# Four residual graph layers on one core: seven-block left products in one more gated step, another split of normalisation and masking between engines

## The chip, the cores and the metric

The kernel runs on one core of a Trainium2 chip. The core has a matrix engine (TensorE, in the profile PE, with its weight loads as PEld), three engines for elementwise work (VectorE or DVE, ScalarE or ACT, GpSimd or POOL) and a queue engine, SyncE or SP, which here issues nearly all DMA transfers. The engines run side by side, each through its own list of instructions in order, and wait for each other by semaphores. The metric is the device time of one launch in microseconds, median of several runs.

## The reference

The input is a batch of 64 graphs, each with 256 nodes of 128 features, and one symmetric 256 x 256 adjacency matrix that they share, all in float32. Four layers follow each other, each as x = layernorm(x + layer(x)):

```
layer 0: h = x Wo; e = leaky(u1[idx1] + u2[idx2]);  att = softmax over rows where adj > 0;  out = att h + x Wself
layer 1: h = x W;  e = leaky(e_src[i] + e_dst[j]);  masked to adj plus the diagonal; softmax; out = elu(att h)
layer 2: five gated steps: m = adj h; z, r = sigmoid(gates of m and h); hv = tanh(w5 m + u5 (r h)); h = (1-z) h + z hv
layer 3: y = x K0 + (adj x) K1 + (adj^2 x) K2 + (adj^3 x) K3, with both adjacency branches equal
```

What matters here: in layer 1, exponentials are multiplied by a mask of zeros and ones before they are used; layer 2 multiplies by the adjacency from the left once in each of its five steps (numbered 0 to 4); each layer ends in a normalisation without learned factors.

## The kernel before

Two graphs make a unit; there are 32 units (`u` from 0 to 31), each with a 128 x 1024 slab of node features in four blocks of 128 nodes x 128 features (two graphs, two node chunks each). Ten lanes of buffers hold ten units at a time. When a unit has gone through all four layers, its lane takes up the next unit.

The order of the work is written by a planner at build time. Every operation is added with an engine and an assumed duration in ns (`add(DVE, 1150, ...)`); the planner plays the engines forward, gives each free engine the ready operation of least rank, and so fixes one list for each engine. The rank is the unit's number times `PERIOD` plus the operation's due time, and the due time grows along the unit's own chain with a factor: `PACE_GATED` in layer 2 and `PACE` in the other layers. The eight PSUM banks are handed out by the same planner. On the chip each engine runs its list in order, however long its operations really take.

Layer 1 (`layer1`) gets the row scores on all partitions by a DMA through DRAM (L543; by transposes for the first three units), makes the scores with ScalarE (L714), takes exponentials over 1024 columns in place (L717), multiplies them by `mask1` (L718, into `p`), and multiplies by X on TensorE (L725).

Layer 2 (`layer2`) needs for each step the left product of the adjacency with the current state. It has two forms. `left` (L771) is four products of 256 columns, two for each graph. `left_fast` gets the same result from seven products of 128 columns, one for each of seven block combinations of the state (built by VectorE at L781, L783, L784 into `s`, which lies in the buffer `e`) and of the matrix (`adjTf`, built once), with products at L788; one product is copied out by ScalarE (L800) and the rest is added up by VectorE at L815, L818, L820 and L821 into `m`. After `left`, ScalarE copies the result to `m` instead (L839). Which steps take which form is in `FAST`, and the step's input must have come in node order by DMA (`far`); of units 0 and 1 and of the last unit some steps do not qualify. The gates (L843) are products of 512 columns, then ScalarE takes tanh (L854, L862, L871) and VectorE combines (L857, L869, L873, L875). VectorE operations with two tensors in SBUF as inputs, such as these four, recur through the whole layer. The new state is turned to node order by a VectorE transpose of 32 x 32 blocks and two sets of DMAs (L883 to L889).

The normalisation (`layernorm`) takes statistics on VectorE (L566, L568), the power -1/2 on GpSimd (L571), and then scales each of the four blocks. From unit `TIGHT` = 4 on, and in the layers of `NORM`, ScalarE does this (L584), for which VectorE prepares a shift (L575, not in layer 0); else VectorE does it (L592, or L588 in layer 0). In layer 3 (`layer3`) the results lie in two PSUM banks, one for each node chunk; the last three units store each chunk by a DMA of its own (L955).

Functions that the change touches, and what calls them:

Of the kernel before, what the change touches and what calls it, by code (L numbers as in the profile page):

```python
# [18 lines left out]
LEAD = 10  # L19
BANKS = 8  # L20
BL = 32
FAST = (2, 3, 4)
NORM = (0, 1, 2, 3)
SCALES = True
TIGHT = 4
FIRST_FAR = {0: 2, 1: 2}
# [1 line left out]
PERIOD = 43e3  # L28
TAIL = 0.3
LATE = 6  # L30
PACE = 2.9
PACE_GATED = 1.56
HOLD = 80
DIRECT_ROWS = 3
# [28 lines left out]
class Plan:  # L63
# [47 lines left out]
    def run(self, spawn, units, key):  # L111
# [22 lines left out]
        def start(lane):  # L134
            mine = [u for u in queue if u % LANES == lane]
            if mine:
# [5 lines left out]
                for t in self.tasks[seen:]:  # L142
                    t.due = max([d.due + (PACE_GATED if t.layer == 2 else PACE) * (d.ns + (
                        d.wait + self.LATENCY["sp" if d.dma else d.eng] if d.dma or d.eng != t.eng else self.OWN[t.eng]))
# [52 lines left out]
def kernel(  # L197
# [28 lines left out]
    nc = tc.nc  # L226
    B, N, D = x.shape
    NC = N // P
    UB = 2
    NU = B // UB  # L230
    T = UB * N
    G = UB * NC
    PE, DVE, ACT, POOL = "pe", "dve", "act", "pool"
# [13 lines left out]
    add = plan.add  # L247

    def bank():
        return Cell(bank=True)  # L250

    def mm_ns(cols, n=1):
        return n * (cols * 1.667 + 5)
# [163 lines left out]
    for t, wT, n in ((wx0, woT, C0), (ws0, wselfT, D + 2)):  # L417
        ps = bank()
# [81 lines left out]
    def bn(ap):  # L500
        return ap.rearrange("p (b n) -> p b n", b=UB)
# [54 lines left out]
                ps.ap[:, g * P : (g + 1) * P], view()[:, g : g + 1].to_broadcast([P, P]), ident.ap), (src, ident), (ps,))  # L556
        return ps, lambda: ps.ap.rearrange("q (b c p) -> q b c p", b=UB, c=NC)

    def layernorm(u, L, pairs, swap=False, centred=False):

        st, ve, rstd = L["st"], L["ve"], L["rstd"]
        sts, xs = object(), object()
        for k, (c, view) in enumerate(pairs):
            add(DVE, 330, lambda k=k, view=view: nc.vector.bn_stats(st.ap[:, k, :], view().rearrange("p j d -> p d j")),  # L566
                (c,), (st,), group=sts)
        add(DVE, 150, lambda: nc.vector.tensor_scalar(  # L568
            ve.ap.rearrange("p (k j) -> p k j", k=2), st.ap.rearrange("p k (j s) -> p k j s", j=2)[:, :, :, 2], 1.0 / D, EPS,
            op0=ALU.mult, op1=ALU.add), (st,), (ve,))  # L570
        add(POOL, 1050, lambda: nc.gpsimd.tensor_tensor(rstd.ap, ve.ap, nhalf.ap, op=ALU.pow), (ve, nhalf), (rstd,))  # L571
        by_act = u >= TIGHT and plan.layer in NORM

        if by_act and not centred:
            add(DVE, 120, lambda: nc.vector.scalar_tensor_tensor(  # L575
                ve.ap.rearrange("p (k j) -> p k j", k=2), st.ap.rearrange("p k (j s) -> p k j s", j=2)[:, :, :, 1], -1.0,
                rstd.ap.rearrange("p (k j) -> p k j", k=2), op0=ALU.mult, op1=ALU.mult), (st, rstd), (ve,))
        for k, (c, view) in enumerate(pairs):
            for j in range(2):
                b, ch = (j, k) if swap else (k, j)  # L580
                at = slice(2 * k + j, 2 * k + j + 1)
                shift, col = (ones, slice(0, 1)) if centred else (ve, at)
                if by_act:
                    add(ACT, 400, lambda j=j, b=b, ch=ch, view=view, at=at, shift=shift, col=col: nc.scalar.activation(  # L584
                        X[u].ap[:, b, ch, :], view()[:, j, :], AF.Identity, bias=shift.ap[:, col], scale=rstd.ap[:, at]),
                        (c, shift, rstd), (X[u],), group=xs)
                elif centred:
                    add(DVE, 260, lambda j=j, b=b, ch=ch, view=view, at=at: nc.vector.tensor_scalar(  # L588
                        X[u].ap[:, b, ch, :], view()[:, j, :], rstd.ap[:, at], 1.0, op0=ALU.mult, op1=ALU.add),
                        (c, rstd), (X[u],), group=xs)  # L590
                else:
                    add(DVE, 260, lambda k=k, j=j, b=b, ch=ch, view=view, at=at: nc.vector.tensor_scalar(  # L592
                        X[u].ap[:, b, ch, :], view()[:, j, :], st.ap[:, k, 3 * j + 1 : 3 * j + 2], rstd.ap[:, at],
                        op0=ALU.subtract, op1=ALU.mult), (c, st, rstd), (X[u],), group=xs)
# [113 lines left out]
    def layer1(u, L):  # L708
        H = D + 1
        esd, e, p = L["esd"], L["e"], L["p"]  # L710
        es, ev = on_all(u, L["m"], L["row"], esd, lambda: esd.ap[:, 0])
        for g in range(G):
            b = g // NC
            add(ACT, 600, lambda g=g, b=b: nc.scalar.activation(  # L714
                e.ap[:, g, :].rearrange("p (c n) -> p c n", c=NC), ev()[:, b], AF.Prelu, bias=esd.ap[:, 1, g : g + 1], alpha=0.2), (es, esd), (e,), group=es)
        ef, pf = e.ap.rearrange("p g n -> p (g n)"), p.ap.rearrange("p g n -> p (g n)")
        add(ACT, 950, lambda: nc.scalar.activation(ef, ef, AF.Exp), (e,), (e,))  # L717
        add(DVE, 1150, lambda: nc.vector.tensor_mul(  # L718
            p.ap.rearrange("p (b c) n -> p b (c n)", b=UB), e.ap.rearrange("p (b c) n -> p b (c n)", b=UB),
            mask1.ap.rearrange("p (o c) n -> p o (c n)", o=1).to_broadcast([P, UB, NC * N])), (e, mask1), (p,))  # L720

        ps_x, px = bank(), L["xT0"]
        for b in range(UB):
            for jc in range(NC):
                add(PE, mm_ns(N), lambda b=b, jc=jc: nc.tensor.matmul(  # L725
                    ps_x.ap[:, b * N : (b + 1) * N], X[u].ap[:, b, jc, :], p.ap[:, b * NC + jc, :],
                    start=(b == 0 and jc == 0), stop=(jc == NC - 1), skip_group_check=True), (X[u], p), (ps_x,))
        add(ACT, 500, lambda: nc.scalar.copy(px.ap, ps_x.ap), (ps_x,), (px,))
        rs, hp, hn, th = L["rs"], L["ht"], L["m"], L["th"]
        ex, parts = L["ex"], object()  # L730
        for b in range(UB):
            ps_o = bank()

            def ov(ps_o=ps_o):
                return ps_o.ap[:, 0 : NC * H].rearrange("p (c k) -> p c k", c=NC)

            for ic in range(NC):
                add(PE, mm_ns(H), lambda b=b, ic=ic, ov=ov: nc.tensor.matmul(  # L738
                    ov()[:, ic, :], bn(px.ap)[:, b, ic * P : (ic + 1) * P], wx1.ap,
                    start=(ic == 0), stop=True, skip_group_check=True), (px, wx1), (ps_o,))  # L740
            r = rs.ap[:, b * NC : (b + 1) * NC].rearrange("p (c o) -> p c o", o=1)
            add(DVE, 120, lambda r=r, ov=ov: nc.vector.reciprocal(r, ov()[:, :, D : D + 1]), (ps_o,), (rs,), group=parts)
            for c in range(NC if SCALES and u >= TIGHT else 0):
                add(ACT, 290, lambda b=b, c=c, ov=ov: nc.scalar.activation(
                    gd(hp.ap)[:, b * NC + c, :], ov()[:, c, 0:D], AF.Copy, scale=rs.ap[:, b * NC + c : b * NC + c + 1]),
                    (ps_o, rs), (hp,), group=parts)
            if not SCALES or u < TIGHT:
                add(DVE, 350, lambda b=b, r=r, ov=ov: nc.vector.tensor_mul(
                    gd(hp.ap)[:, b * NC : (b + 1) * NC, :], ov()[:, :, 0:D], r.to_broadcast([P, NC, D])), (ps_o, rs), (hp,), group=parts)
        if not u:  # L750
            plan.rank = NU
            warm(6, [plan.tasks[-1]])
            plan.rank = None

        add(DVE, 330, lambda: nc.vector.tensor_scalar_min(hn.ap, hp.ap, 0.0), (hp,), (hn,))
        add(ACT, 550, lambda: nc.scalar.activation(th.ap, hn.ap, AF.Tanh, scale=0.5), (hn,), (th,))
        add(ACT, 550, lambda: nc.scalar.activation(ex.ap, hn.ap, AF.Exp), (hn,), (ex,))
        xf = X[u].ap.rearrange("p b c d -> p (b c d)")
        add(DVE, 600, lambda: nc.vector.scalar_tensor_tensor(hp.ap, hp.ap, 0.0, xf, op0=ALU.max, op1=ALU.add),
            (hp, X[u]), (hp,))  # L760
        add(DVE, 600, lambda: nc.vector.scalar_tensor_tensor(th.ap, ex.ap, 1.0, th.ap, op0=ALU.add, op1=ALU.mult),
            (ex, th), (th,))
        add(DVE, 600, lambda: nc.vector.tensor_add(hp.ap, hp.ap, th.ap), (hp, th), (hp,))
        layernorm(u, L, y_pairs(hp))


# [56 lines left out]
    def layer2(u, L):  # L823
        h, ht = turned(u, L, -1), X[u]
        for step in range(STEPS):
            m, at = L["m"], len(plan.tasks)
            fast = step in FAST and far(u, step - 1)
            ps_m = None if fast else bank()
# [94 lines left out]
    def layer3(u, L):  # L923
# [7 lines left out]
        ps = [bank() for _ in range(NC)]  # L931

        def view(c):
            return ps[c].ap.rearrange("p (k b d) -> p k b d", k=2, b=UB)
# [9 lines left out]
        for c in range(NC):  # L944
            for mc in range(NC):
                add(PE, mm_ns(N), lambda c=c, mc=mc: nc.tensor.matmul(  # L946
                    ps[c].ap[:, 0:N], a2T.ap[:, mc, c * P : (c + 1) * P], s.ap[:, mc * N : (mc + 1) * N],
                    start=False, stop=(mc == NC - 1), skip_group_check=True), (a2T, s), (ps[c],))
        layernorm(u, L, [(ps[c], lambda c=c: view(c)[:, 0]) for c in range(NC)], swap=True)
        if u < NU - 3:  # L950
            add("sp", 450, lambda: nc.sync.dma_start(out_u[u], X[u].ap), (X[u],), ())
            return
# [53 lines left out]
```

The softmax here doesn't subtract the row's maximum and nothing guards it: scores larger than these inputs give would overflow.

## Time and profile before

| | |
|---|---|
| device time, median of 3 runs | 1408.14 us (1408.05 to 1408.65) |
| span of the profiled execution | 1406.5 us (this run: 1408.72 us) |
| TensorE clock granted, mean | 0.997 |
| TensorE busy | 1396.0 us, 6163 instructions |
| VectorE busy | 1135.0 us, 2746 instructions |
| ScalarE busy | 939.2 us, 2125 instructions |
| GpSimd busy | 142.4 us, 134 instructions |
| DMA | 146.96 MB, 104 GB/s over the span |

The page gives one profiled execution. A row of the groups reads: line, engine, operation, output and inputs, shapes and count; then the total of its durations in us and the mean of one in ns; then the idle time of that engine just before these operations, and what ended it. Durations of successive operations on one engine overlap a little, so the totals of an engine's rows can exceed its busy time: VectorE starts 512-column operations 0.61 us apart that are recorded with 0.68 us. A float32 product is recorded as two TensorE instructions. A row of waits reads: who waited for whom, us in total, times, the longest. A row of the timeline reads: start, duration, engine, line, operation, and how many in a row.

### The profile page before, as it was taken

The page shows a single profiled execution, that of the slowest core. Times are in us where ns is not written, and L with a number is a line of the kernel's source. Part 1 is how long each engine was busy: PE and PEld are TensorE (multiplying, and loading weights), DVE is VectorE, ACT ScalarE, POOL GpSimd, SP SyncE. Part 2 cuts the span into 40 slices and gives each one's busy share as a digit, 9 for nine tenths or more (in the row PEclk, how much of TensorE's full clock was granted, in tenths as well). Part 3 has the DMA queues.
Part 4 walks back from the last instruction along what each step waited for, and adds up shares of the span by engine and source line. Part 5 has one row for each costly group of instructions (what it writes and reads, how often), then busy time and mean ns, then how long its engine had stood idle before and what let it go on. Part 6 is the DMA issues. An engine that isn't in the chain of part 4 may idle for free.

```text
span 1406.5 us, 20482 instructions
## 1 busy us (share of the span) xinstructions
PE 1396.0 (99%) x6163; PEld 961.8 (68%) x6163; DVE 1135.0 (81%) x2746; ACT 939.2 (67%) x2125; POOL 142.4 (10%) x134
## 2 busy tenths in 40 slices
PE   8999999999999999999999999999999999999998
PEld 8866666676666676676666677676666666666776
DVE  7988888879878788878788788888768888988642
ACT  5797647547766677757677778887766555566454
POOL 0110001001011001011000111021000000101011
PEclk9999999999999999999999999999999999999999
DMA  4213545454554445555445554545554443455411
GB/s 118 61 48 85 120 95 116 100 118 100 132 117 109 97 100 120 121 118 116 99 99 121 126 114 102 114 111 116 116 120 93 107 110 82 116 119 116 110 49 50
DMA packets 533246, 146.96 MB, mean 104 GB/s; under 512 B 460688, under 2 KB 498320, under 8 KB 533136
## 3 DMA queue, kind: packets, MB, share of 16 engines
q1 hardware_dynamic: 532336, 145.13, 46.6%
q8 instruction: 50, 0.82, 0.2%
q14 instruction: 60, 0.49, 0.1%
q10 hardware_dynamic: 800, 0.52, 0.1%
HBM read 81.10 MB, written 64.46 MB: 103 GB/s over the span
## 4 chain that ended last, share of the span: by engine, by line
PE 98%; DVE 1%; ACT 1%; DMA 0%; issue 0%; POOL 0%; SPq 0%; POOLq 0%; ACTq 0%; DVEq 0%
PE ps L843 48%; PE ps L771 12%; PE ps L788 10%; PE ps L939 8%; PE ps L695 4%; PE ps L725 4%; PE ps L946 4%; PE ps L690 2%; PE ps L619 2%; PE ps L738 2%; PE ps L344 0%; DMA m<-row 0%; PE ps L512 0%; PE ps L908 0%; ACT e L714 0%; PE ps L555 0%
## 5 line engine op out<-in xcount | busy, mean ns | idle before, releaser
L843 PE MATMUL ps<-m,gT 128*128 128x512 f32 x960 | 462.4, 593 | 0.4 <-DVE m L821 0.3
L571 POOL TENSOR_TENSOR rstd<-ve,nhalf 128x4 f32<-128x4 f32 x128 | 141.7, 1108 | 1258.9 <-DVE ve L568 1127.3
L843 PEld LDWEIGHTS ps<-m,gT 128*128 128x128 f32 x960 | 173.0, 190 | 124.9 <-issue 102.3
L862 ACT ACTIVATE e<-ps,bias 128x512 f32<-128x512 f32 x160 | 109.9, 688 | 119.4 <-PE ps L843 116.9
L854 ACT ACTIVATE e<-ps,bias 128x512 f32<-128x512 f32 x160 | 109.9, 688 | 84.8 <-PE ps L843 83.7
L843 PE MATMUL ps<-e,u5T 128*128 128x512 f32 x320 | 163.3, 592 | 0.0
L871 ACT ACTIVATE p<-ps,bias 128x512 f32<-128x512 f32 x160 | 109.7, 686 | 41.0 <-PE ps L843 38.5
L771 PE MATMUL ps<-adjT,x 128*128 128x256 f32 x512 | 135.1, 379 | 0.0
L873 DVE SCALAR_TENSOR_TENSOR p<-e,p 128x512 f32<-128x512 f32 x160 | 109.2, 683 | 23.7 <-ACT p L871 22.9
L788 PEld LDWEIGHTS ps<-adjTf,ht 128*128 128x128 f32 x546 | 88.0, 191 | 47.6 <-issue 38.4
L771 PEld LDWEIGHTS ps<-adjT,x 128*128 128x128 f32 x512 | 93.2, 190 | 35.2 <-issue 25.6
L788 PEld LDWEIGHTS ps<-adjTf,e 128*128 128x128 f32 x728 | 95.3, 192 | 15.0 <-issue 12.4
L788 PE MATMUL ps<-adjTf,e 128*128 128x128 f32 x728 | 102.9, 275 | 0.0
L843 PEld LDWEIGHTS ps<-e,u5T 128*128 128x128 f32 x320 | 59.8, 190 | 58.8 <-issue 45.0
L843 PE MATMUL ps<-xT,gT 128*128 128x512 f32 x192 | 97.8, 593 | 0.0
L788 PE MATMUL ps<-adjTf,ht 128*128 128x128 f32 x546 | 91.9, 274 | 0.0
L839 ACT COPY m<-ps 128x512 f32<-128x512 f32 x69 | 40.2, 583 | 70.6 <-PE ps L771 69.7
L857 DVE SCALAR_TENSOR_TENSOR e<-e,xT 128x512 f32<-128x512 f32 x96 | 65.7, 684 | 22.8 <-ACT e L854 22.1
L714 ACT ACTIVATE e<-m,esd 128x256 f32<-128x256 f32 x116 | 83.1, 763 | 0.9 <-DMA m<-row 0.9
L525 DVE STREAM_TRANSPOSE p<-x 128x512 f32<-128x512 f32 x61 | 67.1, 1100 | 15.1 <-ACT x L584 14.7
L695 PEld LDWEIGHTS ps<-ht,p 128*128 128x128 f32 x512 | 66.5, 190 | 12.1 <-issue 11.0
L566 DVE BATCH_NORM_STATS2 st<-ps 128x6 f32<-128x256 f32 x128 | 50.9, 421 | 25.2 <-PE ps L946 19.6
(174 smaller groups left out, 2640.4 us busy)
## 6 DMA issues: line engine op xcount, KB each, us to landing
hb<-p SPq DMA_DIRECT2D x182, 256.0 KB, 2.4
ht<-hb SPq DMA_DIRECT2D x484, 64.0 KB, 2.6
xT<-hb SPq DMA_DIRECT2D x244, 64.0 KB, 2.7
m<-row SPq DMA_DIRECT2D x58, 256.0 KB, 4.0
hb<-p SPq DMA_DIRECT2D x124, 64.0 KB, 1.8
ht<-hb SPq DMA_DIRECT2D x31, 256.0 KB, 3.2
out_dram<-x SPq DMA_DIRECT2D x29, 256.0 KB, 2.5
m<-in_x_dram SPq DMA_DIRECT2D x96, 64.0 KB, 2.7
```

Source lines behind the costliest of these rows:

```text
L525: add(DVE, 1050, lambda: nc.vector.transpose(v.ap.rearrange("p (a g i) -> p g a i", g=G, i=BL), X[u].ap.rearrange("p b c (j a) -> p (b c) ...
L571: add(POOL, 1050, lambda: nc.gpsimd.tensor_tensor(rstd.ap, ve.ap, nhalf.ap, op=ALU.pow), (ve, nhalf), (rstd,))
L695: add(PE, mm_ns(D + 2), lambda b=b, ic=ic, kc=kc, yv=yv: nc.tensor.matmul(yv()[:, ic, :], p.ap[:, b * NC + kc, ic * P : (ic + 1) * P], h.a ...
L714: add(ACT, 600, lambda g=g, b=b: nc.scalar.activation(e.ap[:, g, :].rearrange("p (c n) -> p c n", c=NC), ev()[:, b], AF.Prelu, bias=esd.ap ...
L771: add(PE, mm_ns(N), lambda b=b, mc=mc: nc.tensor.matmul(ps.ap[:, b * N : (b + 1) * N], lhs(b, mc), mat.ap[:, mc, :], start=(mc == 0), stop ...
L788: add(PE, mm_ns(P) + 4, lambda: nc.tensor.matmul(ps.ap[:, at * P : (at + 1) * P], lhs(), mat.ap[:, k, c * P : (c + 1) * P], start=True, st ...
L843: add(PE, mm_ns(T), lambda: nc.tensor.matmul(ps.ap, w(), rhs.ap, start=start, stop=stop, skip_group_check=True), (c, rhs), (ps,), after)
L854: add(ACT, 600, lambda ps_g=ps_g, up=up: nc.scalar.activation(r.ap, ps_g.ap, AF.Tanh, bias=bias2.ap[:, 1:2], scale=0.5 / up), (ps_g, bias2 ...
L862: add(ACT, 600, lambda ps_g=ps_g, up=up: nc.scalar.activation(z.ap, ps_g.ap, AF.Tanh, bias=bias2.ap[:, 0:1], scale=0.5 / up), (ps_g, bias2 ...
L871: add(ACT, 600, lambda ps_v=ps_v, up=up: nc.scalar.activation(v.ap, ps_v.ap, AF.Tanh, bias=bias2.ap[:, 2:3], scale=1 / up), (ps_v, bias2), ...
L873: add(DVE, 600, lambda: nc.vector.scalar_tensor_tensor(v.ap, z.ap, 1.0, v.ap, op0=ALU.add, op1=ALU.mult), (v, z), (v,))
L939: add(PE, mm_ns(N), lambda k=k, src=src, c=c, b=b: nc.tensor.matmul(view(c)[:, :, b, :], bn(src.ap)[:, b, c * P : (c + 1) * P], w3.ap[:, k ...
```

## The change

Five things change; nothing else does.

- `FAST` gains step 1: that step's left product takes the seven-block form wherever its input qualifies, as steps 2, 3 and 4 do already.
- `NORM` loses layer 1: the scaling at the end of layer 1 goes from ScalarE to VectorE in units 4 to 31, and the preparation of a shift for ScalarE goes away there.
- In layer 3 of units 29, 30 and 31 the first of the two node chunks is scaled by VectorE and the second by ScalarE (`last`); before, both were scaled by ScalarE.
- The multiplication by `mask1` in layer 1 goes from VectorE to GpSimd, with an assumed 2300 ns in place of 1150.
- `PACE` goes from 2.9 to 2.8. As the planner orders everything anew, all lists shift. Behind the edit, line numbers are higher by two.

```diff
-FAST = (2, 3, 4)
-NORM = (0, 1, 2, 3)
+FAST = (1, 2, 3, 4)
+NORM = (0, 2, 3)
...
-PACE = 2.9
+PACE = 2.8
...
-    def layernorm(u, L, pairs, swap=False, centred=False):
+    def layernorm(u, L, pairs, swap=False, centred=False, last=False):
...
         for k, (c, view) in enumerate(pairs):
+
+            act = by_act and (k or not last)
             for j in range(2):
...
-                if by_act:
+                if act:
                     add(ACT, 400, lambda j=j, b=b, ch=ch, view=view, at=at, shift=shift, col=col: nc.scalar.activation(
...
-        add(DVE, 1150, lambda: nc.vector.tensor_mul(
+        add(POOL, 2300, lambda: nc.gpsimd.tensor_mul(
             p.ap.rearrange("p (b c) n -> p b (c n)", b=UB), e.ap.rearrange("p (b c) n -> p b (c n)", b=UB),
             mask1.ap.rearrange("p (o c) n -> p o (c n)", o=1).to_broadcast([P, UB, NC * N])), (e, mask1), (p,))
...
-        layernorm(u, L, [(ps[c], lambda c=c: view(c)[:, 0]) for c in range(NC)], swap=True)
+        layernorm(u, L, [(ps[c], lambda c=c: view(c)[:, 0]) for c in range(NC)], swap=True, last=u >= NU - 3)
```

## The prediction

> **What bounds the kernel now.** I read the page first: busy shares, then the chain that ended last.
>
> ```profile
> PE 1396.0 (99%) x6163; PEld 961.8 (68%) x6163; DVE 1135.0 (81%) x2746; ACT 939.2 (67%) x2125; POOL 142.4 (10%) x134
> ...
> PE 98%; DVE 1%; ACT 1%; DMA 0%; issue 0%; POOL 0%; SPq 0%; POOLq 0%; ACTq 0%; DVEq 0%
> ```
>
> TensorE is both the busiest engine and 98% of the chain, so what shortens its instruction stream should shorten the span, unless another engine starts to make it wait. A busy PE is no proof of a PE at its peak, so I then looked at the list of waits for PE alone. It has three entries, 4.0 us together, and one matters:
>
> ```profile
> PE ps L725 <- DVE p L718: 2.3, 1, 2.3
> ```
>
> That is unit 0's mask at 29.7 us. After the first 30 us PE waits once, for 0.3 us. Next, the timeline of PE in the body, for the pitch (start to next start) of the two kinds of left product; the first column is the start, the second the time to the modelled end:
>
> ```profile
> 512.28 1.06 PE L788 MATMUL ps<-adjTf,e 128*128 128x128 f32 x8
> 513.17 0.62 PE L619 MATMUL ps<-wx,xT 128*128 128x133 f32 x4
> ...
> 525.18 1.89 PE L771 MATMUL ps<-adjT,x 128*128 128x256 f32 x8
> 526.91 1.03 PE L771 MATMUL ps<-adjTp,ht 128*128 128x256 f32 x4
> ```
>
> Eight 256-column instructions take 526.91-525.18 = 1.73 us (0.216 each); eight 128-column ones 513.17-512.28 = 0.89 us (0.111 each). Every float32 product of the program is two PE instructions in these records. Then the groups that the change touches:
>
> ```profile
> L771 PE MATMUL ps<-adjTp,ht 128*128 128x256 f32 x240 | 64.9, 379 | 0.0
> L718 DVE TENSOR_TENSOR p<-e,mask 128x1024 f32<-128x1024 f32 x32 | 38.9, 1216 | 4.4 <-ACT e L717 4.4
> L584 ACT ACTIVATE x<-ht,ve,rstd 128x128 f32<-128x128 f32 x112 | 48.9, 485 | 20.4 <-DVE ve L575 20.4
> L571 POOL TENSOR_TENSOR rstd<-ve,nhalf 128x4 f32<-128x4 f32 x128 | 141.7, 1108 | 1258.9 <-DVE ve L568 1127.3
> ```
>
> Last, because work goes to GpSimd, the timeline of POOL and DVE around the longest POOL operation:
>
> ```profile
> 1197.46 3.09 POOL L571 TENSOR_TENSOR rstd<-ve,nhalf 128x4 f32<-128x4 f32 x1 [30.49 <-DVE ve L568]
> ...
> 1197.20 0.68 DVE L873 SCALAR_TENSOR_TENSOR p<-e,p 128x512 f32<-128x512 f32 x1
> 1197.81 0.68 DVE L914 TENSOR_TENSOR m<-ht,x 128x512 f32<-128x512 f32 x1
> 1198.41 0.68 DVE L875 SCALAR_TENSOR_TENSOR p<-p 128x512 f32<-128x512 f32 x1
> 1199.01 0.68 DVE L869 SCALAR_TENSOR_TENSOR p<-e,xT 128x512 f32<-128x512 f32 x1
> ```
>
> This power of 4 elements has a median of 1.007 us; here it took 3.09 us and ended 0.9 us after the fourth of four DVE operations with two SBUF inputs. 31 of the 128 took over 1.1 us, and each of the 31 began beside such a DVE operation.
>
> **What the skill says.** (1) "SBUF — State Buffer", Who interferes with whom: a VectorE instruction with two SBUF inputs and a GpSimd instruction that reads SBUF share a read interface; the one that starts second is blocked until the first ends. The trace agrees for GpSimd waiting (rows above); for VectorE waiting it shows nothing[...]. (2) "GPSIMD Engine Reference", 3.1: a float32 tensor_tensor with two inputs costs about 2.6 cycles an element, 4497 ns for 2048. My estimate from it for 1024 elements: 2.25 us. No row shows one. (3) "TensorE: Matmul & The Clock Gate", Part 1: TensorE falls to half clock after an idle window. The trace agrees: after the 2.26 us wait the eight L725 instructions take 3.23 us, not 1.73.
>
> **The change part by part**, against the profiled span of 1406.5 us; the three timed runs (1408.05 to 1408.65) lie 1.6 to 2.2 us above it, so I take differences in the span and add them to 1408.1.
>
> *Seven-block product at step 1.* Units 0 and 1 keep the old form, so 30 units change, and the built order confirms it: the 120 adjTp products (x240 instructions) all go, the adjTf ones rise by 210. Per unit eight instructions, 1.73 us, become fourteen of 0.111, 1.56 us: 0.17 us less, x30 = 5.1 us. With the pitch of the two groups of four nearby (0.110 to 0.1125) it is 4.7 to 5.7. Fourteen weight loads in place of eight cost nothing further: the 0.111 was measured with them. Since PE is the chain, this counts in full: -5.1.
>
> Beside it VectorE gets seven operations per unit, rows L781, L783, L784, L815, L818, L820, L821: 413+283+284+420+413+281+411 = 2.5 us, x30 = +75.2 us. ScalarE loses 30 copies L839 (583 ns) and gains 30 of L800 (266): -9.5 us.
>
> *Normalisation of layer 1 on VectorE.* ScalarE loses row L584 x<-ht, 48.9 us; VectorE gains 112 of L592 x<-ht at 336 ns, +37.6, and loses 28 of L575 at 153 ns, -4.3. Per unit the path from rstd to X loses a hop and goes from 4 x 0.49 to 4 x 0.34 us; I credit nothing, since PE does not wait there.
>
> *Mask on GpSimd.* VectorE loses 38.9 us; GpSimd gains 32 x 2.25 = 72 us, to 214 us (15%).
>
> VectorE sum: 75.2+37.6-4.3-38.9+2.4 (tail, below) = +72 us of durations. All VectorE rows sum to 1282 us for 1135 busy, as successive operations overlap, so +72 becomes about +64 busy: 1199 us, 86% of 1401. ScalarE falls by about 61 us of durations. VectorE gets close but stays below PE.
>
> *Two-engine normalisation of units 29 to 31.* At the end ScalarE does four L584 in 1.50 us after rstd, then the store. Two go to VectorE (0.40 each, from PSUM), two stay (0.75 us), side by side: about -0.7 on the very end. Bounds 0 and -1.0.
>
> *Start.* Unit 0's exponentials end at 27.49; VectorE was busy with L660 until 28.4 and ended the mask at 29.63. GpSimd is free at 27.5 and ends at about 29.8 to 30: +0.3. Bounds -0.5 and +2, as the half clock may last longer. The two L619 products that now stand before L725 fill part of the wait.
>
> *Queues.* No DMA is added and SP gets the same transfers. On POOL the powers of other units now stand behind 2.25 us masks; ScalarE and VectorE wait for them, with PE two steps away. The planner counts GpSimd at 2.3 us, so it orders around it. PACE 2.8 reshuffles priorities everywhere: no row prices this; I take 0, bounds -1.5 and +2.
>
> *New waits for VectorE.* While a mask reads, the next two-input VectorE operation may be blocked. They fill 669 us of the span, about half, so one comes within some 0.6 us: a block of up to 2.25-0.6 = 1.6 us, x32 = 53 us more on VectorE (then 89% on average). What stands behind it is VectorE's whole queue. From the trace, the time between a VectorE result and the PE instruction that reads it: last add of a seven-block product (L821) to the gate product, median 1.27 us, lower quartile 1.08; reset gate (L857) to its product, median 2.4, lower quartile 1.8. So most blocks are absorbed, some are not. In the likeliest case I charge a few short stalls, +1.2 us; bounds 0 and +11 (below).
>
> Sum: -5.1 -0.7 +0.3 +1.2 = -4.3 us, so 1403.8.
>
> **Rivals.** (A) *GpSimd blocks VectorE and PE pays, slower.* Each block of 1.6 us meets an L821 whose slack is the median 1.27: 0.33 us of stall, x32 = 10.6 us; 1408.1-5.1-0.7+0.3+10.6 = 1413. It decides from 5.5/32 = 0.17 us of PE stall per mask for a loss at all, 0.26 for one of 0.2%. For it: the read interface is shown to be shared, and VectorE is 83 to 88% busy from 100 to 1300 us. Against it: reset gates have more slack, VectorE has idle gaps before L815 and L869 that swallow part, and a mask falls near an L821 only sometimes. (B) *The saving is half eaten.* The 30 new chains of dependent additions and tighter mask results (L718 to L725 had slack under 1.25 us in a quarter of cases) cost PE 0.1 us each, 30+32 times = 6 us less some luck; time about 1407. (C) *The fourteen smaller products save nothing*, because weight loads bound them: 1408. The measured pitch excludes it almost wholly.
>
> **How the numbers follow.** A change below 0.2% (2.8 us) can't be told from none: faster is below 1405.3, slower above 1411.0. Likeliest case 58%, its own range 1401.5 to 1405.3; B with C 18%; A 24%. The range leaves out the far part of A and the luckiest reshuffles: 1400.8 to 1412.5. Faster 0.57, same 0.19, slower 0.24.
>
> **What would show it.** Right: adjTf group at 14 x 121 = 1694 instructions with the 0.111 pitch, adjTp gone from the left products, PE busy near 1391 us, waits of PE still a few us, last ScalarE group of two instead of four. L720's mean on POOL near 2.3 us confirms the price; 3 us and more would mean that it waits for VectorE. Wrong towards A: two-input VectorE rows (L859, L871, L875, L877 after) of 512 columns with maxima near 2 us where before none passed 0.73, and a list of PE waits with tens of entries for m L823, e L859 or p L720. Wrong at the start: a wait of PE at L727 well over 2.3 us.

## The result, and the profile after

The changed kernel is slower: 1424.36 us (median of 4 runs, 1423.15 to 1425.54) against 1408.1 us for the kernel before (4 runs, 1406.73 to 1408.65). The ratio is 1.0117, interval 1.0099 to 1.0134. The forecast was 1403.8, and the time lies outside its range. In what follows lines of the changed kernel are two higher than before (the gate product is L845, the last add of a seven-block product L823, the mask L720).

The page of the changed kernel, span, busy shares, engines of the chain, and three groups:

```profile
span 1423.7 us, 21229 instructions
PE 1401.3 (98%) x6343; PEld 965.8 (68%) x6343; DVE 1226.6 (86%) x3014; ACT 889.0 (62%) x2007; POOL 223.6 (16%) x166
...
PE 78%; DVE 14%; ACT 4%; issue 1%; DMA 1%; SPq 0%; POOLq 0%; DVEq 0%; POOL 0%; ACTq 0%
...
L720 POOL TENSOR_TENSOR p<-e,mask 128x1024 f32<-128x1024 f32 x32 | 79.4, 2483 | 318.9 <-ACT e L719 297.1
L790 PE MATMUL ps<-adjTf,e 128*128 128x128 f32 x968 | 136.0, 275 | 0.0
L790 PE MATMUL ps<-adjTf,ht 128*128 128x128 f32 x726 | 122.9, 274 | 0.0
```

The seven-block products are all there (968+726 = 1694 instructions). But TensorE's part of the chain fell from 98% to 78%, and VectorE now has 14%. The list of TensorE's waits shows where:

```profile
PE ps L845 <- DVE m L823: 5.2, 10, 1.0
PE ps L845 <- DVE e L859: 4.3, 5, 2.9
PE ps L621 <- DVE rs L673: 3.3, 1, 3.3
PE ps L344 <- POOL ident masks.py:199: 1.4, 1, 1.4
PE ps L621 <- DVE xT L608: 1.1, 1, 1.1
```

The first two rows are gate products that wait for a seven-block sum (L823) or a reset gate (L859); the kernel before had one such wait, of 0.3 us. The rows of single lines (nanoseconds: least, median, largest) show VectorE instructions that took up to 2.2 us more than their like, where the kernel before had none, and the mask that they stand beside:

```profile
L859 DVE SCALAR_TENSOR_TENSOR e<-e,xT x96: 642/683/2851, 57.9 to 1394.7; 128x512 f32<-128x512 f32 x96
...
L871 DVE SCALAR_TENSOR_TENSOR xT<-e,p x64: 637/682/2375, 77.8 to 1383.0; 128x512 f32<-128x512 f32 x64
...
L568 DVE TENSOR_SCALAR ve<-st x128: 124/160/1953, 20.9 to 1418.2; 128x4 f32<-128x4 f32 x128
...
L720 POOL TENSOR_TENSOR p<-e,mask x32: 2346/2370/3160, 27.6 to 1284.3; 128x1024 f32<-128x1024 f32 x32
```

One case in full, from the timeline of the changed kernel, engines GpSimd, VectorE and TensorE (start, duration):

```profile
653.84 2.38 POOL L720 TENSOR_TENSOR p<-e,mask 128x1024 f32<-128x1024 f32 x1 [15.12 <-ACT e L719]
...
653.92 2.85 DVE L765 TENSOR_TENSOR ht<-ht,e 128x512 f32<-128x512 f32 x1
656.69 0.41 DVE L820 TENSOR_TENSOR m<-ps,m 128x256 f32<-128x256 f32 x1
657.02 0.67 DVE L871 SCALAR_TENSOR_TENSOR p<-e,xT 128x512 f32<-128x512 f32 x1
657.62 0.28 DVE L822 TENSOR_TENSOR m<-ps,m 128x128 f32<-128x128 f32 x1
657.83 0.67 DVE L875 SCALAR_TENSOR_TENSOR p<-e,p 128x512 f32<-128x512 f32 x1
658.42 0.41 DVE L823 TENSOR_TENSOR m<-ps,m 128x256 f32<-128x256 f32 x1
...
658.89 1.12 PE L845 MATMUL ps<-m,gT 128*128 128x512 f32 x2 [0.65 <-DVE m L823]
```

L765 starts just after the mask, and ends 0.55 us after the mask's end (653.84+2.38 = 656.22; 653.92+2.85 = 656.77): it stood still while the mask ran and then did its own work. The last three additions of the seven-block sum (L820, L822, L823), and two steps of a gate's combination between them (L871, L875), come up to 2.2 us later for it (2.85 less the usual 0.68), and the gate product waits for the last of them.

**Where 17.2 us of the span come from** (1423.7 less 1406.5). Ends of TensorE instructions are modelled, so the list of waits misses part. I therefore took the start of each TensorE instruction against the one before it, and counted as late what exceeds the usual pitch (0.4295 us for 512 columns, 0.216 for 256, 0.111 for 128 to 130) by over 25 ns. The late starts rose from 8.5 to 17.4 us in the first 100 us of the span (+8.9) and from 0.7 to 14.5 us between 100 and 1300 us (+13.8); at the end they fell by 0.3. That is +22.4. The stretch from TensorE's last end to the span's end went from 6.42 to 6.09 us. What is left, 17.2-22.4+0.3 = -4.9, is TensorE's shorter work: the -5.1 of the forecast is there, buried under late starts. The late starts of the first 100 us include what TensorE loses at half clock there (more on this below).

### The profile page after: what moved, and what is told of

Same layout as the page of the kernel before. It is cut to its first block, busy times and chain, and to the rows that moved or that the text cites. A ratio compares the mean times of both kernels' runs of the same rounds, so it can differ in the third digit from the quotient of the medians.

```text
span 1423.7 us, 21229 instructions
## 1 busy us (share of the span) xinstructions
PE 1401.3 (98%) x6343; PEld 965.8 (68%) x6343; DVE 1226.6 (86%) x3014; ACT 889.0 (62%) x2007; POOL 223.6 (16%) x166
## 4 chain that ended last, share of the span: by engine, by line
PE 78%; DVE 14%; ACT 4%; issue 1%; DMA 1%; SPq 0%; POOLq 0%; DVEq 0%; POOL 0%; ACTq 0%
PE ps L845 38%; PE ps L790 10%; PE ps L773 8%; PE ps L941 7%; PE ps L727 4%; PE ps L948 4%; PE ps L697 3%; DVE ht L765 1%; PE ps L740 1%; DVE p L875 1%; ACT e L716 1%; PE ps L692 1%; DVE p L871 1%; PE ps L621 1%; DVE e L859 1%
## 5 line engine op out<-in xcount | busy, mean ns | idle before, releaser
L845 PE MATMUL ps<-m,gT 128*128 128x512 f32 x960 | 466.8, 594 | 5.4 <-DVE m L823 5.2
L845 PEld LDWEIGHTS ps<-m,gT 128*128 128x128 f32 x960 | 172.5, 190 | 132.4 <-issue 99.7
L845 PE MATMUL ps<-e,u5T 128*128 128x512 f32 x320 | 164.7, 598 | 4.5 <-DVE e L859 4.3
L790 PEld LDWEIGHTS ps<-adjTf,ht 128*128 128x128 f32 x726 | 117.6, 191 | 68.3 <-issue 58.3
L790 PEld LDWEIGHTS ps<-adjTf,e 128*128 128x128 f32 x968 | 125.2, 192 | 17.5 <-issue 16.7
L790 PE MATMUL ps<-adjTf,e 128*128 128x128 f32 x968 | 136.0, 275 | 0.0
L720 POOL TENSOR_TENSOR p<-e,mask 128x1024 f32<-128x1024 f32 x32 | 79.4, 2483 | 318.9 <-ACT e L719 297.1
L875 DVE SCALAR_TENSOR_TENSOR p<-e,p 128x512 f32<-128x512 f32 x160 | 109.8, 687 | 16.2 <-ACT p L873 15.4
L790 PE MATMUL ps<-adjTf,ht 128*128 128x128 f32 x726 | 122.9, 274 | 0.0
L845 PEld LDWEIGHTS ps<-e,u5T 128*128 128x128 f32 x320 | 60.0, 191 | 73.3 <-issue 48.7
L845 PE MATMUL ps<-xT,gT 128*128 128x512 f32 x192 | 96.8, 593 | 0.0
L859 DVE SCALAR_TENSOR_TENSOR e<-e,xT 128x512 f32<-128x512 f32 x96 | 68.4, 712 | 19.3 <-ACT e L856 18.6
L817 DVE TENSOR_TENSOR m<-ps,e 128x256 f32<-128x256 f32 x121 | 50.4, 417 | 29.4 <-PE ps L790 27.2
```

Source lines behind the costliest of these rows:

```text
L790: add(PE, mm_ns(P) + 4, lambda: nc.tensor.matmul(ps.ap[:, at * P : (at + 1) * P], lhs(), mat.ap[:, k, c * P : (c + 1) * P], start=True, st ...
L845: add(PE, mm_ns(T), lambda: nc.tensor.matmul(ps.ap, w(), rhs.ap, start=start, stop=stop, skip_group_check=True), (c, rhs), (ps,), after)
L859: add(DVE, 600, lambda h=h: nc.vector.scalar_tensor_tensor(r.ap, r.ap, 1.0, h.ap, op0=ALU.add, op1=ALU.mult), (r, h), (r,))
L875: add(DVE, 600, lambda: nc.vector.scalar_tensor_tensor(v.ap, z.ap, 1.0, v.ap, op0=ALU.add, op1=ALU.mult), (v, z), (v,))
```

## The experiments

The theory after the result: each mask on GpSimd holds VectorE's queue up, and TensorE pays. The rivals: the new order of all lists (the planner's 2300 ns on GpSimd, `PACE`), the larger load of VectorE, or GpSimd's results (the mask, or the powers queued behind it) coming too late for their readers. Of the last, the changed kernel's trace shows nothing for the mask: between 100 and 1300 us no late start stands at its reader, L727, while 12.1 of the 14.5 us stand at gate products L845 that read `m` or `e`. In this section "late starts" are given as two numbers, before and after 100 us (up to 1300).

**The masking left out, lists unchanged.** Edit against the changed kernel:

```diff
-        add(ACT, 950, lambda: nc.scalar.activation(ef, ef, AF.Exp), (e,), (e,))
-        add(POOL, 2300, lambda: nc.gpsimd.tensor_mul(
...
+        add(ACT, 950, lambda: nc.scalar.activation(pf, ef, AF.Exp), (e,), (e,))
+        add(POOL, 2300, lambda: None, (e, mask1), (p,))
```

> The changed kernel with its lists of instructions as they are, but without the masking of layer 1: the exponential writes its result straight to p, and nothing multiplies by the mask (that part of the computation is left out). Theory A (a GpSimd mask blocks VectorE's next two-input operation, and PE pays): the 32 VectorE instructions lengthened by 51.5 us in total vanish, the late starts of PE in the body (14.5 us from 100 to 1300 us) fall below 4 us, the start gains 2 to 6 us, and the time is about 1403 (1399 to 1407). Theory B (the new order and the chains of additions of the seven-block products make PE late): VectorE loses the long instructions, but PE keeps 8 us or more of late starts in the body and the time stays above 1414.

Measured: 1405.02 us (ratio 0.9979, 0.9972 to 0.9987), 19.3 us below the changed kernel; late starts 11.5 / 0.3; no lengthened instruction. The gate products are gone from the list of waits:

```profile
PE ps L621 <- DVE rs L673: 2.1, 1, 2.1
PE ps L344 <- POOL ident masks.py:199: 1.4, 1, 1.4
PE ps L725 <- ACT ht L624: 0.9, 1, 0.9
PE ps L738 <- ACT xT L728: 0.9, 1, 0.9
```

The new order without the mask is not slow, so the order alone is not the cause; 3.0 us of late starts at the beginning (11.5 against 8.5) do come with it. The wait for L673 near 30 us is there without a mask too, at 2.1 us.

**The same lists, the mask issued to VectorE.** The planner still counts it as 2300 ns of GpSimd:

```diff
-        add(POOL, 2300, lambda: nc.gpsimd.tensor_mul(
+        add(POOL, 2300, lambda: nc.vector.tensor_mul(
```

> The changed kernel's plan with all lists as they are, but the mask is issued on VectorE, at the place where the planner put the GpSimd one; the planner gave VectorE no time for it. Theory A: no VectorE instruction is lengthened beside GpSimd, but VectorE is late by 1.2 us at 32 unplanned places in place of 1.6; PE's late starts in the body are about half of 14.5 us (5 to 10), the time 1411 to 1418. Theory B: as the changed kernel or worse, 1422 to 1430, since VectorE's load rises further.

Measured: 1408.03 us (1.0005, 0.9998 to 1.0012), late starts 11.1 / 2.5. So some 1.14 us of VectorE time a mask, which the plan had not foreseen there, cost only 3.0 us over the kernel without masks (2.2 us of late starts after 100 us). Taking the same product from GpSimd back to VectorE wins 16.3 us. This was better than the theory of the block expected; it is what first pointed to a threshold (below).

**The kernel before with its mask on GpSimd.** Lists as before, planned as 1150 ns of VectorE:

```diff
-        add(DVE, 1150, lambda: nc.vector.tensor_mul(
+        add(DVE, 1150, lambda: nc.gpsimd.tensor_mul(
```

> The kernel before with its plan, but the mask is issued on GpSimd; the planner still reserves 1.15 us on VectorE for it. Theory A: about 32 VectorE instructions are lengthened, some 40 to 55 us in total; part falls into the reserved 1.15 us, so PE loses less than in the changed kernel: 1411 to 1420. Theory B: no loss but for the later mask itself (2.4 in place of 1.2 us): 1408 to 1411.

Measured: 1413.42 us (1.0041, 1.0026 to 1.0056), late starts 10.6 / 3.6, 30 lengthened instructions with 48.1 us together. Without any other part of the change the loss is there, though smaller: 48.1 us of standing still go with 2.9 us more of late starts after 100 us, where 51.5 go with 14.2 in the changed kernel. The plan had kept 1.15 us of VectorE for each mask here, and VectorE has less to do; which of the two softens the loss was not tried. Part of the loss is of another kind, the mask's own reader waiting for GpSimd:

```profile
PE ps L725 <- POOL p L718: 3.9, 4, 2.5
```

**The mask cut into four, and into two.** If the block is the cause, shorter GpSimd instructions block less.

```diff
+        def masked():
+            for g in range(G):
+                nc.gpsimd.tensor_mul(p.ap[:, g, :], e.ap[:, g, :], mask1.ap[:, g % NC, :])
+
+        add(POOL, 2300, masked, (e, mask1), (p,))
```

(for two, `range(UB)` and one graph each)

> The changed kernel with the GpSimd mask in four instructions of 256 columns in place of one of 1024, all else as it is. Theory A in its form 'a block is harmful because it is longer than the slack of 1.1 to 1.3 us': four blocks of at most some 0.7 us, PE's late starts in the body fall from 14.5 to under 6 us, the time is 1408 to 1415. If only VectorE's load counts (total blocked time), nothing is gained: 1421 to 1428, or more as the mask lasts longer.

> The changed kernel with the GpSimd mask in two instructions of 512 columns. If blocks hurt by being longer than the slack of 1.1 to 1.3 us, a block of some 1.0 us is near the edge: 1411 to 1417, between four parts (1410.4) and one (1424.4) and nearer to four parts. If the total blocked time counts in proportion, it lies where its blocked time lies between 36 us (four parts) and 52 us (one).

Measured: 1410.35 us (1.002, 1.0012 to 1.0029), late starts 11.6 / 4.9, for four; 1416.36 us (1.0059, 1.0045 to 1.0073), late starts 13.1 / 9.9, for two. The rows of the mask (nanoseconds: least, median, largest; first of four, then of two):

```profile
L722 POOL TENSOR_TENSOR p<-e,mask x128: 715/866/1292, 28.0 to 1271.3; 128x256 f32<-128x256 f32 x128
```

```profile
L722 POOL TENSOR_TENSOR p<-e,mask x64: 1262/1317/2207, 27.6 to 1276.5; 128x512 f32<-128x512 f32 x64
```

Cutting adds GpSimd time (4 x 0.866 = 3.5 us against 2.37) and yet gives 14 us back, so neither a later mask nor powers that queue longer behind it can be the main cause. VectorE instructions lengthened beside a mask: 32 with 51.5 us in the changed kernel, 53 with 41.7 for two, 89 with 35.9 for four.

These runs share their lists, and so show what VectorE time a mask may take. Per mask (divided by 32), against the loss over the kernel without masks: 1.12 us blocked (four), +5.3 us; 1.14 us of its own work (on VectorE), +3.0; 1.30 us blocked (two), +11.3; 1.61 us blocked (one), +19.3. A line of mine through them, 32 x (time - 1.0 us), gives 3.8, 4.5, 9.6 and 19.5. It is a fit over four kernels, and its slope is not to be taken as a price: 5.9 of the 19.3 us fall before 100 us, where half clock adds to them. Nor do two parts tell a threshold from plain proportion to the blocked time, which would put them at 1415.6 us.

The changed kernel's trace shows the threshold mask by mask. Of the 29 masks between 100 and 1300 us, the ten that held VectorE up by 0.52 to 1.46 us are followed by no late start of TensorE within 12 us and before the next mask. Of the 19 that held it up by 1.51 to 2.17 us, 17 are, with 0.49 to 1.35 us each. Over these 17 the block is 1.96 us in the mean and the late start 0.80, so some 1.16 us of a block is absorbed.

**GpSimd for some units only** (`LANES` is 10; the rest on VectorE, lists unchanged).

```diff
+        add(POOL, 2300, lambda: (nc.gpsimd if u >= LANES else nc.vector).tensor_mul(
```

(and `u < LANES` for the other)

> The changed kernel's plan with all lists as they are; the mask is issued on VectorE for the units 0 to 9 and stays on GpSimd for the units 10 to 31 (22 of 32). If PE's loss is 14 us in the body and 6 us in the first 100 us, as the trace of the changed kernel has it, the early part comes back: 1414 to 1419. If the loss goes by the number of GpSimd masks alone (22/32 of 19.4 us above 1405 plus some 1 us for ten on VectorE): 1418 to 1420.

> The other way round: GpSimd for the units 0 to 9, VectorE for 10 to 31, lists as in the changed kernel. By the trace (6 us in the first 100 us, the rest of the ten masks at about 0.45 us each): 1413 to 1418. By number of masks alone (10/32 of 19.4 above 1405, plus 2 us for VectorE's): 1412 to 1414.

Measured: units 10 to 31 on GpSimd, 1417.91 us (1.0074, 1.0058 to 1.009), late starts 11.0 / 13.1; units 0 to 9, 1413.96 us (1.0047, 1.0032 to 1.0062), late starts 17.5 / 4.2. Over the 1408.03 us with all on VectorE that is +9.9 and +5.9, together 15.8 of the 16.3 us: the masks cost each by itself. Each run lies in, or 0.1 us beside, both ranges given for it, so these runs do not decide between the two ways of counting. The late starts split too: those of the beginning go with the first ten units' masks, most of those of the body with the others.

**Step 1 and the tail without the rest.** The kernel before with `FAST = (1, 2, 3, 4)` and `last` only:

```diff
-FAST = (2, 3, 4)
+FAST = (1, 2, 3, 4)
...
-        layernorm(u, L, [...], swap=True)
+        layernorm(u, L, [...], swap=True, last=u >= NU - 3)
```

> The kernel before with two of the five edits alone: the seven-block product at step 1, and the last units' normalisation on two engines. Mask on VectorE, PACE 2.9, layer 1 normalised by ScalarE as before; newly planned. Theory A: nothing blocks VectorE, so the 5.1 us of PE work and about 0.3 to 0.7 us of the end come out in full unless the start shifts: 1401.5 to 1404.5, PE late by no more than 2 us in the body. Theory B (the new chains of additions make PE late): 1406 or more, late starts of over 4 us in the body.

Measured: 1403.28 us (0.9969, 0.9956 to 0.9981), late starts 6.9 / 0.5. The forecast for these two parts, -5.8 us, is a ratio of 0.9959 and lies within the interval. VectorE carries the seven-block form without holding TensorE up. The smaller number at the beginning is not a gain of the edit: this trace has no stretch of half clock near 30 us, where the kernel before has 3.41 us of it, worth 1.7 us by my estimate.

**All of the change but the mask.** The mask planned and issued on VectorE again; then the same with `PACE` as before:

```diff
-        add(POOL, 2300, lambda: nc.gpsimd.tensor_mul(
+        add(DVE, 1150, lambda: nc.vector.tensor_mul(
```

> The changed kernel with the mask on VectorE and planned there (1150 ns): four of the five edits remain, among them the normalisation of layer 1 on VectorE and PACE 2.8. Theory A: no lengthened VectorE instruction, PE late by under 2.5 us in the body, 1402 to 1408; the start decides where in this range. Theory B: VectorE is now the most loaded (about 1240 us busy), so PE is late as in the changed kernel, 1415 or more.

> The changed kernel with the mask planned on VectorE and PACE back at 2.9: what PACE is worth. The kernel with PACE 2.8 has 1402.1. If PACE only reshuffles, 1401 to 1404.5 with the difference at the start (first 45 us of PE); no theory of mine says that it should be worth more than 2 us.

Measured: 1402.14 us (0.9957, 0.9944 to 0.9969), late starts 8.8 / 0.3, faster than both kernels, and the lowest median here, though its interval overlaps that of step 1 and the tail alone. With `PACE` 2.9, 1404.34 us (0.997, 0.996 to 0.998), late starts 8.8 / 1.6: the intervals overlap, so the worth of `PACE` stays open; the traces differ by 1.3 us of late starts after 100 us. Page of the first of them, and the first of the two rows in its list of waits:

```profile
PE 1391.1 (99%) x6343; PEld 963.6 (69%) x6343; DVE 1211.0 (86%) x3046; ACT 883.6 (63%) x2007; POOL 140.5 (10%) x134
```

```profile
PE ps L727 <- DVE p L720: 2.3, 1, 2.3
```

To rule out VectorE's load, the same stretch of both (stretch, its length, then busy us and instructions of PE, PEld, DVE, ACT, POOL, then clock, DMA share, GB/s); first the changed kernel:

```profile
100.00:1300.00 1200.00, 1191.72 (x5343) 804.80 (x5342) 1075.47 (x2591) 760.13 (x1687) 188.39 (x132) 1.00 0.50 109
```

then with the mask on VectorE:

```profile
100.00:1300.00 1200.00, 1200.00 (x5385) 814.48 (x5384) 1075.07 (x2654) 759.95 (x1704) 116.59 (x106) 1.00 0.50 110
```

VectorE is busy for 1075.5 and 1075.1 us of 1200, and TensorE issues 42 instructions more in the second. Of the 1075.5 us, 46.4 are standing still, so VectorE even has more work of its own in the second. It is not how much VectorE has to do, but that it is stopped for longer than the products behind it can bear. Whether a plan that counts these stops as VectorE's time would avoid the loss was not tried.

**Which VectorE operations are stopped.** A kernel of its own that computes nothing of the reference. It runs four operations of one kind, three times with and three times without a mask of 128x1024 that starts just before them; eight kinds in turn (L241 to L248):

```diff
+    kinds = [
+        lambda: nc.vector.scalar_tensor_tensor(c, a, 1.0, b, op0=ALU.mult, op1=ALU.mult),
+        lambda: nc.vector.tensor_mul(c, a, ps),
...
+        lambda: nc.vector.tensor_scalar(s, b[:, 0:4], 1.0, 1.0, op0=ALU.mult, op1=ALU.mult),
+    ]
...
+                    if beside:
+                        nc.gpsimd.tensor_mul(q, e, mask)
+                    nc.vector.transpose(t, d)
+                    for _ in range(4):
+                        kind()
```

> A kernel of its own that computes nothing of the reference: one GpSimd mask of 1024 columns beside a VectorE transpose and four VectorE operations of one kind, eight kinds, three times each, and the same without GpSimd. Theory A: scalar_tensor_tensor with two SBUF inputs (L241): the first of four takes about 2.0 to 2.4 us in place of 0.68, the other three are normal. One input from PSUM (L242), transpose (L243), from PSUM (L245) and reduce (L246) keep their times. For tensor_scalar from SBUF (L244, L247, L248) theory A leaves it open: the changed kernel's list of lengthened instructions has a few L568, so blocks of up to 2 us are expected there too. If GpSimd and VectorE shared the interface by turns instead, all four L241 would be lengthened by a part, and the mask would last much longer than 2.4 us.

Measured, by its rows of single lines (nanoseconds: least, median, largest):

```profile
L241 DVE SCALAR_TENSOR_TENSOR c<-a,b x24: 646/692/2540, 8.0 to 120.0; 128x512 f32<-128x512 f32 x24
L242 DVE TENSOR_TENSOR c<-a,ps x24: 648/686/689, 16.6 to 126.8; 128x512 f32<-128x512 f32 x24
L243 DVE STREAM_TRANSPOSE c<-a x24: 661/711/712, 23.4 to 133.7; 128x512 f32<-128x512 f32 x24
L244 DVE TENSOR_SCALAR c<-a x24: 381/427/2274, 30.3 to 140.6; 128x512 f32<-128x512 f32 x24
L245 DVE TENSOR_SCALAR c<-ps x24: 651/691/692, 36.9 to 147.1; 128x512 f32<-128x512 f32 x24
L246 DVE TENSOR_REDUCE s<-a x24: 640/686/687, 43.7 to 153.9; 128x1 f32<-128x512 f32 x24
L247 DVE TENSOR_SCALAR c<-a x24: 238/285/2074, 50.4 to 159.6; 128x128 f32<-128x128 f32 x24
L248 DVE TENSOR_SCALAR s<-b x24: 123/170/2019, 55.8 to 164.2; 128x4 f32<-128x4 f32 x24
L256 POOL TENSOR_TENSOR q<-e,mask x24: 2341/2344/2355, 11.0 to 161.4; 128x1024 f32<-128x1024 f32 x24
```

Four kinds have a largest of 2 us and more: two inputs in SBUF, and `tensor_scalar` from SBUF at all three sizes. An input in PSUM, the transpose and the reduction are not touched, and the mask itself never gets longer. Only the first of each four is stopped, until the mask's end: the first L241 beside a mask started at 11.39 us and took 2.48; the mask ran from 10.97 to 13.31, and 13.31 plus some 0.56 us of its own work is 13.87. One case from its timeline, of VectorE without and with the mask:

```profile
55.80 0.74 DVE L248 TENSOR_SCALAR s<-b 128x4 f32<-128x4 f32 x4
...
57.09 2.63 DVE L248 TENSOR_SCALAR s<-b 128x4 f32<-128x4 f32 x4
```

Four operations on four elements a partition take 1.9 us more. This is what "SBUF — State Buffer", Who interferes with whom, says in full: not only two SBUF inputs contend with GpSimd, but also those operations (it names `tensor_scalar`) that can enter a mode with both ports. I had used the first half alone; the measurement agrees with both.

## Why the prediction was wrong, point by point

**What held.** The count and pitch of the seven-block products: with the mask on VectorE, the span is 1400.9 us, 5.6 below before; less 0.3 of the stretch after TensorE's last end and 0.4 of fewer late starts, 4.9 us are TensorE's shorter work, for a forecast of 5.1; TensorE is busy for 1391.1 us, as forecast. The price of the mask: 2.37 us median and 2.34 alone, for an estimate of 2.25. The blocked time in all: 1.61 us x 32 = 51.5 us for a forecast of 53. That is in part luck: the forecast took 1.6 us for the most that a block could be, while it is the mean of blocks of 0.52 to 2.17 us.

**The step that failed** is the last term of the sum, "So most blocks are absorbed, some are not", charged at +1.2 us. In the body it was +13.8. Two arguments under it were wrong. First, "a mask falls near an L821 only sometimes". It struck more often than not (17 of 29, below), and where the plan repeats itself, a mask that falls badly does so again: the masks at 653.8, 697.3, 740.8 and 784.2 us stand 43.5 us apart, hold the same L765, and are followed, each 5.05 us later, by the same late gate product. The first was shown above, and these are the rows of the others in the timeline of TensorE:

```profile
702.36 1.12 PE L845 MATMUL ps<-m,gT 128*128 128x512 f32 x2 [0.65 <-DVE m L823]
...
745.81 1.12 PE L845 MATMUL ps<-m,gT 128*128 128x512 f32 x2 [0.63 <-DVE m L823]
...
789.27 1.13 PE L845 MATMUL ps<-m,gT 128*128 128x512 f32 x2 [0.89 <-DVE m L823]
```

Their late starts are 0.92, 0.92, 0.90 and 1.16 us. 13.6 of the body's 14.5 us begin within 12 us after a mask; 17 of the 29 masks there cost 0.49 to 1.35 us, the other 12 nothing. Not all of the plan repeats: the distance from mask to mask goes from 6 to 82 us. Second, the discount. The median slack of 1.27 us against a block of 1.6 gave rival A 0.33 us a mask, and I then took most of that off for idle gaps that would swallow some. The slack was not far wrong: at the 17 masks some 1.16 us are absorbed, between the lower quartile (1.08) and the median that I had read. But the gaps swallowed no more than that, and one size for all blocks hid the long ones, 1.96 us in the mean of the 17. Rival A had the right mechanism and stood at 1413, just outside the range of 1400.8 to 1412.5 that I gave; it was itself too mild, at 0.33 a mask against 13.6/29 = 0.47 in the body.

**The second mis-sized term** is the start: +0.3, with a bound of +2. It measured +8.9. I had looked only at when unit 0's mask would be ready (29.8 to 30 us; it ended at 29.97), not at what it holds up. Timeline of VectorE and TensorE in the changed kernel:

```profile
28.59 1.40 DVE L668 TENSOR_TENSOR nm<-nm,s 128x4 f32<-128x4 f32 x1
...
30.74 1.25 PE L621 MATMUL ps<-wx,xT 128*128 128x133 f32 x4 [3.26 <-DVE rs L673]
...
49.97 1.87 DVE L640 TENSOR_TENSOR d<-u 128x2 f32<-128x2 f32 x1
...
55.34 2.39 DVE L628 SCALAR_TENSOR_TENSOR cu<-cu 128x4 f32<-128x4 f32 x2
...
58.67 2.08 PE L845 MATMUL ps<-e,u5T 128*128 128x512 f32 x2 [2.92 <-DVE e L859]
```

Unit 0's mask (27.63 us) holds L668, an operation on four elements, until 29.99; the masks at 49.47 and 55.35 hold L640 and L628. TensorE then waits 3.26 and 2.92 us, and in each wait its clock falls to half. The windows of the first stretches show it in the clock, the third figure from the right; changed kernel:

```profile
30.00:40.00 10.00, 8.75 (x42) 7.75 (x43) 5.18 (x18) 5.10 (x17) 0.00 (x0) 0.66 0.19 34
40.00:60.00 20.00, 17.09 (x96) 13.43 (x96) 19.92 (x56) 13.00 (x31) 8.21 (x5) 0.95 0.16 40
60.00:100.00 40.00, 40.00 (x181) 28.74 (x181) 32.20 (x97) 37.02 (x105) 4.67 (x4) 0.94 0.21 49
```

A mean of 0.66 over 10 us is 6.8 us at half speed, and 0.95 and 0.94 make another 6.8 or so across 60 us. Before, there was one such stretch of 3.4 us, at 30 us, and none after it until the last 5 us. My estimate of what half clock adds to the +8.9 us is half of the 10.2 us more of it, 5.1 us at most.

"TensorE: Matmul & The Clock Gate", Part 1, puts the fall to half clock after about 3.4 us of idling; here waits of 2.92 and 3.26 us went with it, and 2.26 us in the kernel before, so a shorter wait than the page's figure can be enough. It need not be: with step 1 and the tail alone TensorE waits 2.26 us at the same place, and no half clock follows. In all twelve traces of these kernels the clock changes only at whole multiples of 3.413 us after its first rise (in the changed kernel it rises at 6.68 us, then changes at 30.57, 37.40, 57.88 and 64.70), so how a wait lies to these moments may decide; no run tested that.

Of the +8.9 us, 3.0 come with the order alone (kernel without masks), the rest with the first ten units' masks. The stretch at 30 us is among the 3.0: without masks it lasts as long as in the changed kernel (30.20 to 37.02 us), 3.41 us more than before, worth 1.7 us by the same estimate. The one at 58 us is not there without masks. The other 1.3 us stay open.

**Smaller points.** The tail was put at -0.7. The stretch after TensorE's last end is 6.42 us before, 6.09 after, 6.08 with the mask on VectorE, but 6.48 with step 1 and the tail alone: a gain of that edit is not shown. VectorE's busy time was put at 1199; without a mask it is 1179.5 us, after the change 1226.6, as a stopped instruction counts as busy. I had expected tens of waits for L823, L859 and L720; the list has 15, while 17 masks alone are followed by late starts, as modelled ends hide the small waits. Layer 1 out of `NORM` shows no gain and no loss of its own: 1403.28 us without it, 1402.14 and 1404.34 with it. Rival B's 6 us did not come: after 100 us the kernels with the mask planned on VectorE have 0.3 to 1.6 us of late starts, against 0.7 before. The reading that each of the 31 slow powers before began beside an operation with two SBUF inputs misses two: those at 76.46 and 122.62 us began while of the two kinds only a `tensor_scalar` from SBUF ran (L663, L755; in the first case an operation with two SBUF inputs began 0.09 us later). So the kind of operation that the prediction left out may have shown in its own trace. Rival C is excluded by 1403.28.

## What to carry to other kernels

Work given to GpSimd is not free for VectorE: price it by the time that VectorE's whole queue stands still behind the first operation that needs the shared interface. Take the spread of these stops and not their mean, and set it against the slack to the bounding engine: here stops up to 1.46 us cost nothing, and of those from 1.51 us on nearly all did. Where a plan repeats itself, ask in which phase the new instruction falls, for it will hit the same instruction again. If VectorE has room, leave the work there: the rest of the change with the mask on VectorE had the lowest time of all. If GpSimd must take it, cut it small: four instructions in place of one took half as much GpSimd time again and gave back 14 of 19 us.

## What the runs showed that I had not expected

- A `tensor_scalar` on four elements a partition, 0.17 us by itself, took 2.02 us beside a mask; in the changed kernel L568, of this kind, shows a largest of 1953 ns. Not only operations with two tensors wait.
- In the isolated test the mask, first to start, is never the one to wait (2341 to 2355 ns in 24 cases). In the changed kernel it can be: at 927.58 us it took 2.91 us, 0.54 over its median, beside an L761 (two SBUF inputs) from 927.59 to 928.27 that took its usual 0.68; then the next such operation, L763, took 2.19 us, 1.51 of them standing still.
- The loss grows faster than the block: 1.12, 1.30 and 1.61 us of it a mask gave 5.3, 11.3 and 19.3 us, of which 4.6, 9.6 and 14.2 us are late starts after 100 us.
